# A state-space and attention kernel: softplus as one ScalarE function over three tiles in PSUM, and two changes to the order of work

## The chip, the core and the metric

The kernel runs on one core of one Trainium2 chip. The core has five engines that run side by side, each with its own queue of instructions in fixed order: TensorE (PE in the profile), VectorE (DVE), ScalarE (ACT), GpSimd (POOL) and SyncE (SP, which here only starts DMA transfers). The metric is the device time of one execution in microseconds (us). Three runs of the kernel before took 4100.95, 4101.35 and 4101.04 us, median 4101.04.

## The reference

The input is a batch of 8 images of 384 channels and 32 x 32 pixels, that is 1,024 positions. Layer 0 normalises each position over the channels, runs a selective state-space model (Mamba) forwards and backwards along the positions with the same weights, adds a gated depthwise 3 x 3 convolution, and adds the input. Layer 1 is causal attention with six heads over the 1,024 positions, and a feed-forward with sign-binarised weights and 8-bit scaling by groups of the batch. The groups cover five of the eight images; the feed-forward adds nothing for the rest.

What the change touches is delta, the step width of the state-space model:

```
dt, Bm, Cm = jnp.split(x_dbl, [dt_rank, dt_rank + D_STATE], axis=-1)
delta = jax.nn.softplus(jnp.einsum('blr,dr->bld', dt, dt_proj_w) + dt_proj_b)
A = -jnp.exp(A_log)
deltaA = jnp.exp(delta[..., None] * A)
deltaBu = (delta * u)[..., None] * Bm[:, :, None, :]
# step: h = dA * h + dBu; y = sum over 16 states of h * c
```

softplus(x) is log(1 + exp(x)). The rank of dt is 24, the number of states is 16, and everything is computed in 32-bit floats.

## The kernel before, in words

Channels lie on the 128 partitions in three chunks (`c`), positions along the free dimension in two halves of 512 (`h`), and `d` is the direction. A tile of 128 x 512 floats fills one of the eight banks of PSUM. One bank is for sums of the scan (`ps_y`), two for the scan's decay factors (`ps_da`), and five (`ps_any`) are shared by all else. In SBUF, ten tiles of 128 x 1,024 (`mid`) and six of three times that size (`big`) are shared in turn.

**The stages.** For each batch element `before_scan` (L639) normalises, projects, convolves, applies Silu, keeps u and the rows of B and C in DRAM, and computes the gates and the local convolution. Its last steps are the deltas (L903). For each of the four pairs of direction and half (`parts_of`) and each chunk, a delta step loads u from DRAM, makes one matmul of 25 rows (24 of dt, one that brings in the bias) into a bank `dp`, and works out softplus as max(x, 0) + log(1 + exp(-|x|)), with a correction for what is lost when 1 is added to a small number. That takes six instructions of ScalarE (Abs, Exp, add 1, Ln, a copy of w = 1 + e into the bank, and a copy of the result to SBUF) and four of VectorE. It then writes delta (`dl`) and delta times u (`ud`) to DRAM. There are 12 such steps for one batch element and 96 in all.

The scan itself is cut into units (L940): one unit is two blocks of 32 channels times 4 states for one chunk, one pair of direction and half, 96 units for one batch element. A unit (`s_first`, `s_scan`, `s_sum`) is a GpSimd multiplication of `scan_ud` and a row of B into `scan_g` (six buffers), then twice an Exp on ScalarE into `ps_da` and a recurrence on VectorE, a ScalarE copy of the last column (`scan_carry`) in half of the units, a GpSimd multiplication by the row of C, and TensorE sums over the states into `ps_y`. When all units of a chunk are through, `s_gate` puts u, the two directions and z together. Then come attention (L1068) and, for five batch elements, the feed-forward (L1375).

**What sets the order.** The code doesn't call the engines directly. Each call is recorded as an operation with a rank, which is its number in the order of recording, less an offset (`hurry`); a `together` block is recorded as one operation, so its instructions stand one behind another on their engine. `place` (L246) then plays the operations through with estimated costs: at each moment an engine takes the ready operation of the lowest rank whose tiles can be given a place. What comes out is the fixed order of every engine's queue. Waits on the chip follow from data and buffers. All instructions are emitted at L364, so the profile shows this line for nearly all; tiles tell them apart.

The order of recording comes from the end of the function. `slots` (L1505) records the scan's units with an offset of 600. `spread_over` (L1493) merges lists of steps, each with a weight in us, by the share of its list's weight that lies ahead of a step. The first batch element's first part runs alone (`lead`). The rest of it, the second and third elements' `before_scan` and the binarising of the weights are merged with the first units. From then on a cycle is attention of element i, then its feed-forward merged with `before_scan` of element i + 3 (L1571). The units are laid over this sequence so that an element's units are through before its attention.

[...] The kernel keeps the set named in `LOG_EXP` (L52), which has Exp and Ln; wherever it uses Silu, Tanh or Gelu, it records them together and asks for `LOG_EXP` again right after (L861, L1425).

Of the kernel before, what the change touches and what calls it, by code (L numbers as in the profile page):

```python
# [22 lines left out]
HB = 512  # L23
# [3 lines left out]
RANK = 24  # L27
# [13 lines left out]
DW = BC0 + 2 * NS  # L41
# [10 lines left out]
LOG_EXP = "natural_log_exp_and_others"  # L52
# [108 lines left out]
class Plan:  # L161
# [15 lines left out]
    @contextmanager  # L177
    def together(self):
        self.group = []
        yield  # L180
        self.group = None

    @contextmanager
    def hurry(self, offset):
        self.sooner += offset
        yield
        self.sooner -= offset
# [58 lines left out]
    def place(self):  # L246
        engines = self.ENGINES
        waiting = {e: [] for e in engines}
        ready = {e: [] for e in engines}
        free_at = {e: 0.0 for e in engines}  # L250
        count = itertools.count()
# [42 lines left out]
        while events:  # L294
            now = events[0][0]
            while events and events[0][0] <= now:
                heapq.heappop(events)
            moved = True
            while moved:
                moved = False  # L300
                for e in engines:
                    while waiting[e] and waiting[e][0][0] <= now:
                        op = heapq.heappop(waiting[e])[2]
                        if op.start is None:
                            heapq.heappush(ready[e], (op.rank, next(count), op))
                    while free_at[e] <= now and ready[e]:
                        aside, op, held = [], None, set()
                        while ready[e]:
                            item = heapq.heappop(ready[e])
                            if item[2].start is not None:  # L310
                                continue
                            if fits(item[2], now, held):
                                op = item[2]
                                break
                            aside.append(item)
                        for item in aside:
                            heapq.heappush(ready[e], item)
                        if op is None:
                            break
                        op.name, op.start, moved = e, now, True  # L320
                        for t in op.tiles:
                            if t.place is None:
                                k = t.kind
                                k.free.sort()
                                t.place = k.free.pop(0)[1]
                        if op.dma:
                            free_at[e] = now + 0.06
                            dma_free = max(dma_free, now + 1.2) + op.time
                            op.end = dma_free + 1.2
                        else:  # L330
                            op.end = free_at[e] = now + op.time
                        heapq.heappush(events, (free_at[e], next(count), e))
                        done.append(op)
                        for t in op.tiles:
                            users_left[id(t)] -= 1
                            if not users_left[id(t)]:
                                at = max(u.end for u in t.users) + self.SIGNAL
                                t.kind.free.append((at, t.place))
                                t.kind.freed += 1
                                heapq.heappush(events, (at, next(count), e))  # L340
                        for nxt in op.behind:
                            nxt.left -= 1
                            if not nxt.left:
                                release(nxt)
# [33 lines left out]
def kernel(  # L378
# [21 lines left out]
    nc = plan = Plan(tc, homes)  # L400
    together, hurry = plan.together, plan.hurry
# [6 lines left out]
    dram = Pool(plan, "dram", 5, DRAM)  # L408
    ps = Pool(plan, "ps", 1, PSUM)

    def ctile(name, shape, dt=F32):
        return const.tile(shape, dt, name=name, tag=name)
# [4 lines left out]
    def mtile(name, n=L):  # L417
        return mid.tile([P, n], F32, name=name, tag="mid")
# [6 lines left out]
    def bank(name, tag=None):  # L425
        tag = tag if tag in BANKS else "any"
        return ps.tile([P, HB], F32, name=name, tag=tag, bufs=BANKS[tag])

    def parts_of(b):
        return LAST_PARTS if b == ORDER[-1] else PARTS  # L430

    def half(h):
        return slice(h * HB, (h + 1) * HB)

    def chunk(c):
        return slice(c * P, (c + 1) * P)

    def load(dst, src):
        nc.sync.dma_start(out=dst, in_=src)
# [8 lines left out]
    spilled = {}  # L448
# [16 lines left out]
    wdt = ctile("wdt", [P, C])  # L465
    for d in range(2):
        nc.scalar.dma_start(out=wdt[d * DW : d * DW + RANK, :], in_=w_dt)
        nc.scalar.dma_start(
            out=wdt[d * DW + RANK : d * DW + RANK + 1, :],
            in_=vecs[:, V_DTB : V_DTB + 1].rearrange("c o -> o c"),  # L470
# [19 lines left out]
    nc.vector.tensor_copy(cmask[:, HB - P :], masked)  # L490
    onesc = ctile("onesc", [P, P])
    nc.gpsimd.memset(onesc, 1.0 / C)
    onecol = ctile("onecol", [P, 1])
    nc.gpsimd.memset(onecol, 1.0)
    eps = ctile("eps", [P, 2])
    nc.gpsimd.memset(eps[:, 0:1], 1e-6)
    nc.gpsimd.memset(eps[:, 1:2], 1e-5)
# [141 lines left out]
    def before_scan(b, tags, emit, later=None, diags=None, lead=None):  # L639


        st = {}
        turns = itertools.cycle(tags)

        def bank_of(name):
            return bank(name, next(turns))
# [253 lines left out]

        def delta(c, d, h):  # L903
            ew = mtile(f"ew{d}_{b}_{c}_{h}").rearrange("p (i l) -> p i l", i=2)
            du = mtile(f"du{d}_{b}_{c}_{h}").rearrange("p (i l) -> p i l", i=2)
            e, w, dl, u = ew[:, 0, :], ew[:, 1, :], du[:, 0, :], du[:, 1, :]
            load(u, spilled[b, "u", d, c][:, half(h)])
            dp = bank_of(f"dp{d}_{b}_{c}_{h}")
            r = slice(d * DW, d * DW + RANK + 1)
            nc.tensor.matmul(  # L910
                out=dp, lhsT=wdt[r, chunk(c)], rhs=st["xd"][r, half(h)], start=True, stop=True
            )
            nc.scalar.activation(e, dp, AF.Abs)
            nc.scalar.activation(e, e, AF.Exp, scale=-1.0)
            nc.scalar.activation(w, e, AF.Identity, bias=onecol)
            nc.scalar.activation(dl, w, AF.Ln)

            nc.vector.scalar_tensor_tensor(dl, dp, 0.0, dl, ALU.max, ALU.add)
            nc.scalar.copy(dp, w)
            nc.vector.scalar_tensor_tensor(dp, dp, 1.0, e, ALU.subtract, ALU.subtract)  # L920
            nc.vector.tensor_tensor(dp, dl, dp, ALU.subtract)
            nc.vector.tensor_tensor(u, u, dp, ALU.mult)
            nc.scalar.copy(dl, dp)
            for i, what in enumerate(("dl", "ud")):
                t = dram.tile([P, HB], F32, name=f"s{what}_{d}_{b}_{c}_{h}", tag=f"sp_{what}_{d}_{c}_{h}")
                nc.sync.dma_start(out=t, in_=du[:, i, :])
                spilled[b, what, d, c, h] = t

        for d, h in parts_of(b):
            for c in range(NC):  # L930
                to = lead if lead is not None and (d, h) == (0, 0) else emit
                to(lambda c=c, d=d, h=h: delta(c, d, h), 3.0)

# [556 lines left out]
    class Gap(float):  # L1490
        pass

    def spread_over(*lists):  # L1493

        keyed = []
        for k, steps in enumerate(lists):
            total, at = sum(us for _, us in steps), 0.0
            for f, us in steps:
                keyed.append(((at + us / 2) / total, k, (f, us)))
                at += us  # L1500
        return [e[2] for e in sorted(keyed, key=lambda e: e[:2])]

# [22 lines left out]
    def run(*lists):  # L1525
        for f, _ in spread_over(*lists):
            f()

    def steps_of(stage, *args, **kwargs):
        out = Steps()  # L1530
        stage(*args, out, **kwargs)
        return out
# [31 lines left out]
    rest, later, due = [], list(ORDER[1 + ahead :]), [(0.0, 0)]  # L1564
    for i, b in enumerate(ORDER):
        if i > 0:
            due.append((sum(us for _, us in rest), i * per))
        fed = Steps()
        rest += steps_of(attention, b, fed) if i < B - 1 else []
        if fed and later:  # L1570
            fed = spread_over(fed, steps_of(before_scan, later.pop(0), ("pt", "pt", "av")))  # L1571
            fed = [(f, JOINT * (SHORT if isinstance(us, Gap) else us)) for f, us in fed]
        rest += fed
        if i == B - 2:
            late, early = Steps(), Steps()
            attention(ORDER[-1], Steps(), late, early)
            due.append((sum(us for _, us in rest), i * per + 3 * per // len(PARTS)))
            rest += early
# [7 lines left out]
    at = 0.0  # L1586
# [61 lines left out]
```

## Time and profile before

| | |
|---|---|
| median of three runs | 4101.04 us |
| profiled execution | 4101.66 us |
| its span, first to last instruction | 4099.8 us |
| mean granted TensorE clock | 0.894 |
| PE, DVE busy | 3414.5, 3458.9 us |
| ACT, POOL busy | 2687.2, 3577.0 us |
| DMA | 612.03 MB, 149 GB/s |
| first multiplication of GpSimd for the scan | 74.7 us |
| last one ends | 3921 us |

The span is that of one profiled execution; the execution's own time is 1.9 us longer. Busy time of an engine is the time in which it executes; the rest it waits, for data, for a buffer or for the instruction ahead in its own queue. Rows of groups read: line, engine, operation, output from inputs (partitions x elements), count, then busy time in us and mean in ns of one, and after the second bar the time that the engine stood idle just ahead of these instructions, and for whom. Rows of waits read: engine, waiting tile, whom it waited for, total us, number of waits, longest.

### The profile page before, as it was taken

Reading aid. Unit: us, or ns where it says so; the run is one execution under the profiler, and the core shown is the slowest. Engines: PE = TensorE matmul, PEld = TensorE weight load, DVE = VectorE, ACT = ScalarE, POOL = GpSimd, SP = SyncE. Lnnn points to the kernel's source line nnn. Section 1 sums busy time; section 2 is a strip of 40 time slices with the busy share of each in tenths; the row PEclk is TensorE's granted clock in tenths of the full one; section 3 lists DMA queues with packets and bytes.
Section 4 is the critical chain, followed back from the end, with each engine's and each line's share of the span. In section 5 each row is a group of like instructions: output and inputs, shape, how many; then the busy total and the mean of one; then the engine's idle time right before and its main releaser. Section 6 shows DMA issues by size and latency. Waiting matters only on the chain. (4 is left out here: it accounts for less than half of the span.)

```text
span 4099.8 us, 43593 instructions
## 1 busy us (share of the span) xinstructions
PE 3414.5 (83%) x12426; PEld 1336.9 (33%) x12426; DVE 3458.9 (84%) x4867; ACT 2687.2 (66%) x5288; POOL 3577.0 (87%) x1560
## 2 busy tenths in 40 slices
PE   4557387989889898979998798987989879998999
PEld 1112022433323333324333243332433323333344
DVE  5999999888898889988899977999788998877843
ACT  5856767586674867657666667666586665856635
POOL 3999999999799997989998899978899788999920
PEclk8678596999979999889999899997999979999999
DMA  5635655333374344543345633447324464233300
GB/s 195 218 134 189 237 176 209 131 108 133 136 243 146 104 142 146 196 166 115 127 140 174 223 114 115 136 143 268 114 79 133 148 240 169 96 128 110 133 26 31
DMA packets 338971, 612.03 MB, mean 149 GB/s; under 512 B 34617, under 2 KB 93417, under 8 KB 338729
## 3 DMA queue, kind: packets, MB, share of 16 engines
q1 hardware_dynamic: 329072, 593.10, 42.0%
q10 hardware_dynamic: 9656, 16.15, 1.1%
q8 instruction: 98, 1.61, 0.2%
q14 instruction: 145, 1.18, 0.1%
HBM read 456.03 MB, written 153.09 MB: 149 GB/s over the span
## 5 line engine op out<-in xcount | busy, mean ns | idle before, releaser
L364 POOL TENSOR_TENSOR scan_g<-scan_g,scan_bc 128x1024 f32<-128x1024 f32 x768 | 1814.8, 2368 | 199.3 <-ACT scan_carry L364 116.8
L364 POOL TENSOR_TENSOR scan_g<-scan_ud,scan_bc 128x1024 f32<-128x1024 f32 x768 | 1820.0, 2377 | 140.5 <-DMA scan_ud<-dram_sp_ud 68.4
L364 ACT ACTIVATE ps_da<-scan_dl,const_amat 128x512 f32<-128x512 f32 x1536 | 1050.2, 689 | 702.1 <-DVE scan_g L364 688.5
L364 DVE TENSOR_TENSOR_SCAN scan_g<-ps_da,scan_carry,scan_g 128x512 f32<-128x512 f32 x768 | 943.3, 1267 | 99.1 <-POOL scan_g L364 81.2
L364 DVE TENSOR_TENSOR_SCAN scan_g<-ps_da,scan_g 128x512 f32<-128x512 f32 x768 | 898.0, 1208 | 108.4 <-POOL scan_g L364 83.5
L364 PE MATMUL ps_any<-big_big,mid_mid 128*128 128x512 f32 x2016 | 940.9, 619 | 38.5 <-DVE big_big L364 18.4
L364 PE MATMUL ps_y<-scan_g,const_gather 128*32 128x512 f32 x3072 | 477.6, 698 | 299.7 <-POOL scan_g L364 293.9
L364 PEld LDWEIGHTS ps_any<-big_big,mid_mid 128*128 128x128 f32 x2016 | 384.9, 197 | 598.0 <-issue 481.0
L364 PE MATMUL ps_any<-big_big,big_big 128*128 128x512 f32 (+4 forms) x1728 | 558.6, 560 | 22.3 <-ACT ptp_ptn L364 7.4
L364 PE MATMUL ps_any<-const_ident,mid_mid 128*128 128x128 f32 x1728 | 306.7, 306 | 61.9 <-DVE small_nm L364 25.2
L364 DVE CUSTOM_DVE_ANT_0 mid_mid<-ps_any,const_cmask 128x512 f32<-128x512 f32 (+3 forms) x576 | 292.2, 547 | 59.5 <-PE ps_any L364 58.9
L364 PEld LDWEIGHTS ps_any<-big_big,big_big 64*128 64x128 f32 (+1 forms) x1728 | 226.9, 190 | 322.3 <-issue 202.2
L364 DVE SCALAR_TENSOR_TENSOR ps_any<-big_big,const_vec,ps_any 128x496 f32<-128x496 f32 (+6 forms) x420 | 303.2, 727 | 19.1 <-ACT ps_any L364 5.5
L364 PEld LDWEIGHTS ps_any<-const_ident,mid_mid 128*128 128x128 f32 x1728 | 200.1, 150 | 283.8 <-issue 89.1
L364 ACT COPY ptp_ptn<-ps_any 128x512 f32<-128x512 f32 (+3 forms) x576 | 256.2, 478 | 48.9 <-PE ps_any L364 41.1
L364 ACT ACTIVATE mid_mid<-mid_mid,small_low 128x512 f32<-128x512 f32 (+3 forms) x384 | 242.8, 635 | 53.5 <-DVE small_low L364 52.9
L364 PE MATMUL ps_any<-ptp_ptn,big_big 128*64 128x512 f32 (+3 forms) x1152 | 260.6, 532 | 13.1 <-ACT ptp_ptn L364 11.8
L364 PEld LDWEIGHTS ps_y<-scan_g,const_gather 128*32 128x32 f32 x3072 | 64.5, 115 | 595.1 <-POOL scan_g L364 499.4
L364 PE MATMUL ps_any<-mid_mid,const_wdt 25*128 25x512 f32 x192 | 155.3, 939 | 81.5 <-ACT mid_mid L364 51.6
L364 ACT ACTIVATE mid_mid<-mid_mid 128x512 f32<-128x512 f32 (+1 forms) x261 | 188.8, 738 | 3.9
L364 ACT COPY mid_mid<-ps_any 128x512 f32<-128x512 f32 x234 | 134.6, 581 | 79.3 <-DVE mid_mid L364 38.0
L364 PE MATMUL ps_any<-mid_mid,const_onesc 128*128 128x512 f32 x252 | 135.2, 665 | 57.7 <-ACT mid_mid L364 45.3
(106 smaller groups left out, 3467.6 us busy)
## 6 DMA issues: line engine op xcount, KB each, us to landing
scan_ud<-dram_sp_ud SPq DMA_DIRECT2D x384, 256.0 KB, 3.6
scan_dl<-dram_sp_dl SPq DMA_DIRECT2D x384, 256.0 KB, 3.5
scan_bc<-dram_rows SPq DMA_DIRECT2D x256, 256.0 KB, 3.2
scan_us<-dram_sp_u SPq DMA_DIRECT2D x96, 256.0 KB, 2.6
mid_mid<-dram_sp_u SPq DMA_DIRECT2D x96, 256.0 KB, 4.6
dram_sp_ud<-mid_mid SPq DMA_DIRECT2D x96, 256.0 KB, 3.7
dram_sp_dl<-mid_mid SPq DMA_DIRECT2D x96, 256.0 KB, 3.2
dram_sp_u<-mid_mid SPq DMA_DIRECT2D x42, 512.0 KB, 5.1
```

Source lines behind the costliest of these rows:

```text
L364: getattr(engine, what)(*[mapped(v) for v in args], **{k: mapped(v) for k, v in kwargs.items()})
```

## The change

There are four parts.

1. `delta` becomes `deltas`, one step for three chunks: three loads of u and three matmuls into three banks; then, as one `together` group with an offset of 60, three Softplus activations in place in the banks and the request for `LOG_EXP`; then for each chunk one VectorE multiplication by u, one ScalarE copy and the two transfers to DRAM. The tile `ew` and the constant `onecol` go. A step's weight is 6.0 for three chunks, where it was 3.0 for each.
2. In `place`, an operation of any engine but TensorE that touches a PSUM tile which already has its place is queued with a rank lower by 60.
3. `spread_over` can multiply the shares of all lists but the first by a factor `sooner`.
4. The merge of the feed-forward with the later element's `before_scan` uses `sooner=0.8`.

```diff
@@ place
                         if op.start is None:
-                            heapq.heappush(ready[e], (op.rank, next(count), op))
+                            opened = e != "tensor" and any(
+                                t.place is not None and t.kind.space == PSUM for t in op.tiles
+                            )
+                            heapq.heappush(ready[e], (op.rank - 60 * opened, next(count), op))
@@ before_scan
-        def delta(c, d, h):
-            ew = mtile(f"ew{d}_{b}_{c}_{h}").rearrange("p (i l) -> p i l", i=2)
-            du = mtile(f"du{d}_{b}_{c}_{h}").rearrange("p (i l) -> p i l", i=2)
-            e, w, dl, u = ew[:, 0, :], ew[:, 1, :], du[:, 0, :], du[:, 1, :]
-            load(u, spilled[b, "u", d, c][:, half(h)])
-            dp = bank_of(f"dp{d}_{b}_{c}_{h}")
-            r = slice(d * DW, d * DW + RANK + 1)
-            nc.tensor.matmul(
-                out=dp, lhsT=wdt[r, chunk(c)], rhs=st["xd"][r, half(h)], start=True, stop=True
-            )
-            nc.scalar.activation(e, dp, AF.Abs)
-            nc.scalar.activation(e, e, AF.Exp, scale=-1.0)
-            nc.scalar.activation(w, e, AF.Identity, bias=onecol)
-            nc.scalar.activation(dl, w, AF.Ln)
-
-            nc.vector.scalar_tensor_tensor(dl, dp, 0.0, dl, ALU.max, ALU.add)
-            nc.scalar.copy(dp, w)
-            nc.vector.scalar_tensor_tensor(dp, dp, 1.0, e, ALU.subtract, ALU.subtract)
-            nc.vector.tensor_tensor(dp, dl, dp, ALU.subtract)
-            nc.vector.tensor_tensor(u, u, dp, ALU.mult)
-            nc.scalar.copy(dl, dp)
...
+        def deltas(d, h):
+            st_of = []
+            for c in range(NC):
+                du = mtile(f"du{d}_{b}_{c}_{h}").rearrange("p (i l) -> p i l", i=2)
+                load(du[:, 1, :], spilled[b, "u", d, c][:, half(h)])
+                dp = bank_of(f"dp{d}_{b}_{c}_{h}")
+                r = slice(d * DW, d * DW + RANK + 1)
+                nc.tensor.matmul(
+                    out=dp, lhsT=wdt[r, chunk(c)], rhs=st["xd"][r, half(h)], start=True, stop=True
+                )
+                st_of.append((c, du, dp))
+            with hurry(offset=60), together():
+                for _, _, dp in st_of:
+                    nc.scalar.activation(dp, dp, AF.Softplus)
+                nc.scalar.preload_act_table_set(LOG_EXP)
+            for c, du, dp in st_of:
+                dl, u = du[:, 0, :], du[:, 1, :]
+                nc.vector.tensor_tensor(u, u, dp, ALU.mult)
+                nc.scalar.copy(dl, dp)
...
         for d, h in parts_of(b):
-            for c in range(NC):
-                to = lead if lead is not None and (d, h) == (0, 0) else emit
-                to(lambda c=c, d=d, h=h: delta(c, d, h), 3.0)
+            to = lead if lead is not None and (d, h) == (0, 0) else emit
+            to(lambda d=d, h=h: deltas(d, h), 6.0)
@@ spread_over
-    def spread_over(*lists):
+    def spread_over(*lists, sooner=1.0):
...
-                keyed.append(((at + us / 2) / total, k, (f, us)))
+                share = (at + us / 2) / total
+                keyed.append((share * sooner if k else share, k, (f, us)))
@@ the cycles
-            fed = spread_over(fed, steps_of(before_scan, later.pop(0), ("pt", "pt", "av")))
+            fed = spread_over(fed, steps_of(before_scan, later.pop(0), ("pt", "pt", "av")), sooner=0.8)
```

More of the change, by code (lines that the diff above doesn't have):

```diff
@@ L492 @@
     nc.gpsimd.memset(onesc, 1.0 / C)
-    onecol = ctile("onecol", [P, 1])
-    nc.gpsimd.memset(onecol, 1.0)
     eps = ctile("eps", [P, 2])
@@ L899, in _ @@
                 spilled[b, "rows", d] = rows
-        def delta(c, d, h):
-            ew = mtile(f"ew{d}_{b}_{c}_{h}").rearrange("p (i l) -> p i l", i=2)
-            du = mtile(f"du{d}_{b}_{c}_{h}").rearrange("p (i l) -> p i l", i=2)
-            e, w, dl, u = ew[:, 0, :], ew[:, 1, :], du[:, 0, :], du[:, 1, :]
-            load(u, spilled[b, "u", d, c][:, half(h)])
-            dp = bank_of(f"dp{d}_{b}_{c}_{h}")
-            r = slice(d * DW, d * DW + RANK + 1)
-            nc.tensor.matmul(
-                out=dp, lhsT=wdt[r, chunk(c)], rhs=st["xd"][r, half(h)], start=True, stop=True
-            )
-            nc.scalar.activation(e, dp, AF.Abs)
-            nc.scalar.activation(e, e, AF.Exp, scale=-1.0)
-            nc.scalar.activation(w, e, AF.Identity, bias=onecol)
-            nc.scalar.activation(dl, w, AF.Ln)
-            nc.vector.scalar_tensor_tensor(dl, dp, 0.0, dl, ALU.max, ALU.add)
-            nc.scalar.copy(dp, w)
-            nc.vector.scalar_tensor_tensor(dp, dp, 1.0, e, ALU.subtract, ALU.subtract)
-            nc.vector.tensor_tensor(dp, dl, dp, ALU.subtract)
-            nc.vector.tensor_tensor(u, u, dp, ALU.mult)
-            nc.scalar.copy(dl, dp)
[L924 to L927, printed above, removed]
@@ new lines, in deltas @@
+        def deltas(d, h):
[17 more added lines that the diff above has]
+                nc.scalar.copy(dl, dp)
+                for i, what in enumerate(("dl", "ud")):
+                    t = dram.tile(
+                        [P, HB], F32, name=f"s{what}_{d}_{b}_{c}_{h}", tag=f"sp_{what}_{d}_{c}_{h}"
+                    )
+                    nc.sync.dma_start(out=t, in_=du[:, i, :])
+                    spilled[b, what, d, c, h] = t
```

## The prediction

> **What bounds the kernel now.** I read the busy shares first, then the busy time by stage, then who makes GpSimd wait, then the groups of instructions that the edit touches, and last the start of the run.
>
> ```profile
> PE 3414.5 (83%) x12426; PEld 1336.9 (33%) x12426; DVE 3458.9 (84%) x4867; ACT 2687.2 (66%) x5288; POOL 3577.0 (87%) x1560
> POOL 3999999999799997989998899978899788999920
> ```
>
> No engine is full, and three are near it. GpSimd (POOL) runs the two multiplications of every scan unit, 1,536 of them; the slices say that it is full in long stretches and has dips. By stage (columns: busy us, with instruction counts, of PE, weight loads, DVE, ACT, POOL; then TensorE clock, DMA share, GB/s):
>
> ```profile
> 75.00:740.00 665.00, 414.88 (x1142) 127.47 (x1141) 616.24 (x737) 457.87 (x779) 632.73 (x274) 0.72 0.54 189
> 740.00:3450.00 2710.00, 2365.11 (x8470) 931.90 (x8469) 2376.53 (x3252) 1813.55 (x3509) 2469.50 (x1062) 0.92 0.44 151
> 3450.00:3921.00 471.00, 429.79 (x1988) 183.62 (x1987) 371.10 (x624) 304.13 (x723) 465.65 (x202) 0.96 0.35 120
> 3921.00:4100.00 179.00, 168.95 (x768) 80.57 (x766) 67.64 (x206) 79.17 (x227) 0.54 (x1) 1.00 0.08 26
> ...
> 1150.00:1250.00 100.00, 77.93 (x192) 25.95 (x191) 94.52 (x115) 69.76 (x116) 88.89 (x40) 0.76 0.75 260
> 1250.00:1350.00 100.00, 94.66 (x358) 40.56 (x356) 81.43 (x132) 57.73 (x134) 94.44 (x41) 0.99 0.38 130
> ```
>
> The end is: head (75 us until POOL's first multiplication), POOL's 3,568 us, the idle time in between, and 179 us after its last one. So POOL's idle time is what can be won: 665.00 - 632.73 = 32 us in the first stage, 2,710.00 - 2,469.50 = 240 us in the five cycles of attention, feed-forward and before_scan, 5 us after 3,450. The fifth row is a stretch with twelve delta steps: DVE is at 95% and POOL at 89%, and PE falls to 78% at a clock of 0.76. A stretch of attention (750 to 950 us) has POOL idle for 0.4 us only. Who makes POOL wait between 740 and 3,450 us:
>
> ```profile
> POOL scan_g L364 <- ACT scan_carry L364: 104.4, 51, 13.8
> POOL scan_g L364 <- PE ps_y L364: 62.4, 25, 7.6
> POOL scan_g L364 <- DVE scan_g L364: 59.4, 34, 9.1
> ```
>
> The first and third are one thing: the scan of a unit (Exp on ACT, recurrence on DVE, a copy of the carry on ACT) is late. The second is PE: the sums that free scan_g stand behind other matmuls.
>
> **What the Trainium skill says.** "Perfetto Trace Analysis", section Optimization Strategy, says that a kernel can have several regimes, each with its own most contended engine; the rows above agree (DVE first in the delta stretch, POOL in attention, PE in the tail). "ScalarE activation tables", section What a function is on this engine, says that the same operands cost the same whichever function's table is read; the trace agrees for Exp and Ln (one row, 628 ns) and doesn't show Softplus. "ScalarE: Activation LUTs", section What ACT_TABLE_LOAD costs, gives 1,283 ns for a load and about as much again for a drain; here a load takes 1,283 ns, and at 103.40 us the next ACTIVATE starts 1.30 us after it, so I count no drain. "TensorE: Matmul & The Clock Gate", section What's actually happening, says that idle stretches halve the array's clock; the delta row's 0.76 against 0.99 right after agrees.
>
> **The change part by part.** The rows concerned, of all 96 delta steps (the first also holds nothing else: 96 Exp and 96 Ln):
>
> ```profile
> L364 ACT ACTIVATE mid_mid<-mid_mid 128x512 f32<-128x512 f32 x192 | 120.5, 628 | 3.7
> L364 ACT ACTIVATE mid_mid<-mid_mid,const_onecol 128x512 f32<-128x512 f32 x96 | 69.1, 720 | 2.4 <-PE ps_any L364 0.9
> L364 ACT ACTIVATE mid_mid<-ps_any 128x512 f32<-128x512 f32 x96 | 56.5, 588 | 25.5 <-PE ps_any L364 13.9 <-DVE ps_any L364 7.8 <-DMA big_big<-dram_sp_gy 3.7
> L364 ACT COPY ps_any<-mid_mid 128x512 f32<-128x512 f32 x96 | 55.6, 580 | 22.1 <-DVE mid_mid L364 21.8
> L364 ACT ACT_TABLE_LOAD x67 | 86.0, 1283 | 1.8 <-PEq L1635 0.7
> L364 DVE TENSOR_TENSOR ps_any<-mid_mid,ps_any 128x512 f32<-128x512 f32 x96 | 66.6, 694 | 2.9
> L364 DVE SCALAR_TENSOR_TENSOR ps_any<-ps_any,mid_mid 128x512 f32<-128x512 f32 x96 | 65.4, 681 | 8.4 <-ACT ps_any L364 7.8
> ```
>
> DVE: three of four operations go: 0.694 + 0.681 + 0.677 (max and add, the row of mid_mid from ps_any and mid_mid) = 2.052 us a step, 24.6 us a batch, 197 us in all. ACT: Abs 0.588, Exp and Ln 2 x 0.628, Identity 0.720, copy into the bank 0.580 = 3.144 us go; one Softplus comes, never seen in the trace. Bounds 0.55 to 0.72, the cheapest and dearest 512-wide form; I take 0.578, what Exp over a bank in place (ps_any from ps_any) takes. Three steps save 7.70 us and get two table loads, 2.57: net 5.13 us a group, 20.5 a batch, 164 in all. The loads are a choice too: the diff reloads the log-and-exp set itself, so Softplus lies in another; if it didn't, 82 us of ACT more would be saved.
>
> Matmuls, the 96 loads of u and the 192 spills on SP stay; the three loads of a group now stand ahead of its six spills. One mid tile a step goes (ew), which only relieves its ten buffers. Three of the five shared banks are held together; I cost it at nothing, because the old steps already overlapped (at 1,201 us one step's Abs runs ahead of the last copy of the one before) and each bank is held for no longer than the old chain's 6 us; without that cover, a group holds back the next bank user for its 4.3 us. The removed memset is 0.1 us under the loads at the start.
>
> *Head.* Before, POOL's first load stands on SP behind the third step's dl spill:
>
> ```profile
> 70.51 0.32 SPq L364 DMA_DIRECT2D dram_sp_dl<-mid_mid  x1
> 70.92 2.46 SPq L364 DMA_DIRECT2D scan_ud<-dram_sp_ud  x4
> 74.70 11.59 POOL L364 TENSOR_TENSOR scan_g<-scan_ud,scan_bc 128x1024 f32<-128x1024 f32 x5 [61.64 <-DMA scan_ud<-dram_sp_ud]
> ```
>
> The six matmul records of the three steps end at 56.4. After: last Softplus 57.0, reload 58.3, three copies 59.9, spill 60.3, load landing 3.8 later: 64.3 instead of 74.7. Of these 10 us I take 8, as the first units then meet the next batch's convolutions on DVE.
>
> *First stage.* 33 more steps take 68 us of DVE out of 665; POOL can win at most its 32 us. I take half: 15 us.
>
> *Five cycles.* A cycle has 240 / 5 = 48 us of POOL idle. About 10 stand behind the four Gelu of 2.85 us (waits of 9.4 and 13.8 us at two of them), which stay; 12 are PE's ps_y. The twelve delta steps' stretch and the 100 us after it hold 17 to 28 us of the idle (11 + 6 in the rows shown). DVE loses 24.6 us of work there; I put it at 20 us of POOL idle a cycle: 100 us. Bounds: 0 (the scans then wait for ACT or PE) and 26 (all but Gelu and PE): 130.
>
> *New bursts.* A group blocks ACT for 1.28 + 3 x 0.58 + 1.28 = 4.3 us, and queued behind it are a unit's Exp and carry copy, for which DVE and then POOL wait. A Silu burst of 4.2 us at 103.40 costs POOL nothing (no idle from 98 to 185 us). The Gelu burst of 13.7 us cost 9.4, so some 4 us are covered. Where DVE is behind already, the cover is gone: 0 to 4.3 us each. I take 0.5 x 32 = 16 us.
>
> *Planner and placing.* An operation that reads or writes a bank already given gets 60 ranks; scans stand 600 ahead, so it mainly reorders evictions among the rest: 0, bounds -15 (banks sooner free for PE) to +15. The before_scan list counts 180 us of weight before and 168 after, with deltas in its last 36 and 24; with the factor 0.8 they move from shares 0.80 to 1.00 of the feed-forward to 0.69 to 0.80, and the convolutions and gates ahead of them are packed tighter, where DVE is full (184.5 of 200 us from 950 to 1,150). What DVE saves pays for it: 0, bounds -20 to +40. SP's loads and spills of the moved steps move along; a batch's deltas are ready before its scan in either case (the last spill of a delta is issued at 3,394 us).
>
> *Tail.* PE is busy for 169 of 179 us; nothing there is edited: 0.
>
> Sum: -8 - 15 - 100 + 16 = -107 us. The profiled execution took 4,101.66 us for a span of 4,099.8; span 3,993, execution 3,995. The median of the runs is 0.6 below the profiled one: **3,994 us**.
>
> **The rivals.** *Only off the path* (B): POOL's waits in the delta stretch pass to PE's sums and to the bursts; what is left is head, half the first stage and 5 us a cycle, 8 + 8 + 25 = 41 us: 4,060 (4,045 to 4,092). For it: 62 us of waits are PE's, and PE already runs at 87% over the cycles; against: PE loses 22 us in the delta row for want of ACT and DVE. *Slower* (C): the bursts. They fall where DVE is behind, so each stalls POOL by its length and delays the next scan; from 3.8 us a group (123 / 32) on they eat the gain, and with the tighter placing at its +40 it ends near 4,140 (4.3 x 32 + 40 - 123 = +55 at most). For it: the waits of 9.4 and 13.8 us behind Gelu; against: the Silu burst at 103. *More* (D): the rest of the work also gets ahead of the scans, so that part of the last batch's early half leaves the tail; 60 us in the first stage and 25 a cycle are there for it, and 179 us can lose some 60: 3,915. *Not what it says*: Softplus without loads, or the planner not moving the list; it changes the sum by less than 40 us and lies in A.
>
> **How the numbers follow.** My forecast (A, 3,945 to 4,045) has 0.60, B 0.18, D 0.08, C 0.11, and no difference 0.03. Within 0.2%, 8 us, is about what can't be told from no change. Faster is A, B and D: 0.86. The range leaves out C, no change and the lower half of D, 0.18: 3,925 to 4,092, which also takes in the bounds of the cycles and of the placing.
>
> **What would show it.** Softplus of about 0.58 us x96 and 131 table loads; DVE near 3,262 and ACT near 2,523 us; POOL's first multiplication near 65 us; POOL idle from there to its last below 200 us (now 277), with the fall in the delta stretches; the tail at 179. I am wrong if POOL's waits on scan_carry grow, with table loads right ahead of them, or if ps_y waits take what DVE's gave up.

## The result, and the profile after

The changed kernel takes 4044.70 us (median of four runs, 4043.55 to 4048.24), where the kernel before takes 4101.19 us beside it (4100.95 to 4103.24). The ratio is 0.9863, with a 95% interval of 0.9846 to 0.9880: 56.5 us faster, about half of the 107 us forecast. The time lies at the edge of the forecast's own range and inside the wider one. The profiled execution took 4048.24 us with a span of 4046.4 us, 53.4 us below the span before.

The busy shares and GpSimd's slices after:

```profile
PE 3387.3 (84%) x12426; PEld 1330.0 (33%) x12426; DVE 3264.4 (81%) x4580; ACT 2546.6 (63%) x4967; POOL 3570.8 (88%) x1559
POOL 2999999999999999789998799987899997999910
```

DVE fell by 194.5 us (forecast 197). The slices show where GpSimd gained: the first 7 stands in slice 17 of 40, where it stood in slice 11; later dips remain. By stage, with the limits of the stages 50 to 60 us sooner, as the work behind the first stage is (columns as in the prediction):

```profile
75.00:690.00 615.00, 423.81 (x1170) 140.05 (x1171) 527.91 (x615) 393.28 (x644) 594.76 (x258) 0.75 0.59 202
690.00:3400.00 2710.00, 2343.55 (x8486) 923.10 (x8485) 2275.17 (x3093) 1733.96 (x3324) 2511.85 (x1083) 0.92 0.45 152
3400.00:3861.00 461.00, 405.86 (x1920) 169.10 (x1919) 359.47 (x611) 300.68 (x715) 455.37 (x197) 0.96 0.35 116
3861.00:4047.00 186.00, 174.91 (x782) 83.16 (x780) 69.12 (x209) 79.26 (x227) 0.28 (x1) 1.00 0.07 25
...
1090.00:1190.00 100.00, 95.85 (x263) 35.06 (x262) 72.99 (x80) 53.78 (x82) 100.00 (x44) 0.91 0.75 259
```

GpSimd's idle time in the first stage is 615.00 - 594.76 = 20 us (before 32), in the five cycles 2,710.00 - 2,511.85 = 198 us (before 240), and behind 3,400 us 461.00 - 455.37 = 6 us: 224 us in all, where the prediction's sign was "below 200". In the delta stretch of the first cycle, the fifth row, the bound moved as forecast: DVE 73 us where it had 95, GpSimd full, the TensorE clock 0.91 where it was 0.76. In the later cycles most of what is won there is lost again, as shown below. GpSimd's waits between 690 and 3,400 us:

```profile
POOL scan_g L367 <- PE ps_y L367: 90.7, 22, 12.5
POOL scan_g L367 <- ACT scan_carry L367: 54.5, 36, 8.1
POOL scan_g L367 <- DVE scan_g L367: 38.7, 21, 10.9
```

The lateness of the scan (second and third rows) fell from 163.8 to 93.2 us. The wait for PE's sums rose from 62.4 to 90.7 us: 28 of the 71 us came back as another wait.

To see when this happens I split GpSimd's timeline by batch element, 192 multiplications each, and added up the idle time ahead of them (us). In the first element's sum, some 62 us are the wait for the first load in both kernels.

| | el. 0 | 1 | 2 | 3 | 4 | 5 | 6 | 7 | sum |
|---|---|---|---|---|---|---|---|---|---|
| idle before | 82 | 12 | 47 | 54 | 44 | 49 | 51 | 0 | 339 |
| idle after | 80 | 2 | 15 | 43 | 50 | 48 | 42 | 3 | 283 |
| of it for ps_y, before | 0 | 0 | 6 | 20 | 13 | 15 | 13 | 0 | 67 |
| of it for ps_y, after | 3 | 0 | 0 | 23 | 24 | 28 | 18 | 0 | 96 |

42 of the 56 us are won in elements 1 and 2, which are scanned from 538 to 1,446 us. From element 3 on, the idle time is what it was, and the wait for ps_y makes up more of it. The length of a cycle agrees: from the first Gelu to the fifth it takes (3,238.0 - 1,089.8) / 4 = 537 us before and (3,211.1 - 1,054.7) / 4 = 539 us after. GpSimd's last multiplication ends at 3,861.3 us instead of 3,921.5, and what follows it takes 185.1 instead of 178.3 us: -60.2 + 6.8 = -53.4 us, the difference of the spans.

### The profile page after: what moved, and what is told of

Its sections match the earlier page's. It is cut to its first block, busy times and chain, and to the rows that moved or that the text cites. A ratio compares the mean times of both kernels' runs of the same rounds, so it can differ in the third digit from the quotient of the medians.

```text
span 4046.4 us, 42961 instructions
## 1 busy us (share of the span) xinstructions
PE 3387.3 (84%) x12426; PEld 1330.0 (33%) x12426; DVE 3264.4 (81%) x4580; ACT 2546.6 (63%) x4967; POOL 3570.8 (88%) x1559
## 5 line engine op out<-in xcount | busy, mean ns | idle before, releaser
L367 PE MATMUL ps_any<-big_big,mid_mid 128*128 128x512 f32 x2016 | 952.9, 625 | 78.4 <-DVE big_big L367 56.5
L367 PE MATMUL ps_y<-scan_g,const_gather 128*32 128x512 f32 x3072 | 467.8, 686 | 275.1 <-POOL scan_g L367 265.0
L367 PE MATMUL ps_any<-mid_mid,const_wdt 25*128 25x512 f32 x192 | 132.1, 852 | 41.6 <-DVE mid_mid L367 32.2
L367 DVE COPY big_big<-ps_any 128x512 f32<-128x512 f32 (+1 forms) x86 | 54.2, 631 | 128.6 <-PE ps_any L367 128.6
```

Of the source, the lines that this page charges most:

```text
L367: getattr(engine, what)(*[mapped(v) for v in args], **{k: mapped(v) for k, v in kwargs.items()})
```

## The experiments

Each kernel was run beside the kernel before; times are medians. "Idle" is GpSimd's idle time counted as above. A kernel with another edit also gets another order of its queues from `place`; what that alone can do is measured below (29 us), and differences under it can't be laid to an edit.

**Which part carries it.** Four kernels take the change apart. `d_only` has the Softplus part alone; its edits of the changed kernel:

```
- heapq.heappush(ready[e], (op.rank - 60 * opened, next(count), op))
+ heapq.heappush(ready[e], (op.rank - 0 * opened, next(count), op))
...
- fed = spread_over(fed, steps_of(before_scan, later.pop(0), ("pt", "pt", "av")), sooner=0.8)
+ fed = spread_over(fed, steps_of(before_scan, later.pop(0), ("pt", "pt", "av")), sooner=1.0)
```

> The kernel after with only its first part: Softplus over three tiles, no lowering of ranks, factor 1.0. Theory PACK (the factor 0.8 packs before_scan ahead of Gelu, where DVE is full, and loses there what Softplus saves behind it): about 4,015 us, 30 faster than after, the distance from one Gelu to the next near 525 us instead of 537 to 539. Theory PACE (the cycle of 537 us is set by something that neither Softplus nor the order touches, such as the pace of the scans): 4,045 us, distance unchanged. Theory HELP (rank and factor each add to the gain): 4,060 us or more.

`d_opened` has Softplus and the ranks (the second of these edits alone), `d_sooner` has Softplus and the placing (the first alone):

> The kernel after with the factor 1.0 instead of 0.8. PACK: 4,010 to 4,020 us, GpSimd's waits for PE's sums fall from 97 us toward 67, the windows with PE below 35 of 50 us ahead of Gelu go. PACE: 4,045 us. HELP: 4,055 us.

> The kernel after without the lowering of ranks for taken banks. PACK and PACE: 4,045 us within 10, the ranks only reorder evictions. HELP: 4,055 us or more.

`order_only` is the kernel before with both changes of order and the old delta steps:

> The kernel before with both order changes (ranks lower by 60 on taken banks, factor 0.8) and its own softplus. PACK: slower than before, 4,115 to 4,130 us, since the packing has nothing to pay for it. PACE: 4,100 us. HELP: 4,080 us.

| kernel | us | ratio to before, 95% |
|---|---|---|
| d_only | 4050.19 | 0.9873, 0.9860 to 0.9887 |
| d_opened | 4049.59 | 0.9870, 0.9856 to 0.9883 |
| d_sooner | 4074.41 | 0.9930, 0.9917 to 0.9944 |
| order_only | 4111.22 | 1.0020, 1.0013 to 1.0027 |

Softplus alone gives 52 of the 56.5 us; with both changes of order in place on either side (`order_only` against the changed kernel) it gives about 65. The two changes of order bring 5 us on top, which the intervals can't tell from nothing; without Softplus they cost 9. Beside Softplus the ranks alone change nothing in the time, and the factor alone costs 24 us. The prediction's nought for the two, with bounds from -35 to +55, stands. None of the three theories in these expectations has the time right in all four; PACE has the unchanged distance from one Gelu to the next right, 538 us in `d_only`.

**Where Softplus acts.** `d_first` uses the new delta steps for the first three batch elements only, `d_later` for the other five only (with `not in` for `in`); the rest keeps the old `delta`. Both are edits of `d_only`:

```
- to(lambda d=d, h=h: deltas(d, h), 6.0)
+ if b in ORDER[:3]:
+     to(lambda d=d, h=h: deltas(d, h), 6.0)
+     continue
+ for c in range(NC):
+     to(lambda c=c, d=d, h=h: delta(c, d, h), 3.0)
```

> Softplus over three tiles for the first three batch elements only, the old delta steps for the other five; order of work as before. The prediction's own sum gives 8 + 15 - 6 = 17 us for these: about 4,085. Theory FRONT (the five later cycles give nothing, because PE's waits take over there what DVE and ACT give up; the gain is all in the part before the cycles): 4,055 us, nearly the whole 52 of the first part alone.

> The opposite: old delta steps for the first three elements, Softplus for the other five. The prediction's sum: 100 - 10 = 90 us faster, 4,012. FRONT: within 12 us of before, 4,090 to 4,100.

`d_first` takes 4069.89 us, 31.9 below before (ratio 0.9921, 0.9909 to 0.9934); `d_later` 4092.48 us, 9.3 below (0.9977, 0.9968 to 0.9986). Idle in elements 0 to 2 is 106 us with `d_first` (before 141) and 143 with `d_later`; in elements 3 to 7 it is 199 and 192 (before 198). In these runs 60 of the 96 steps, those of the five cycles, gain 9 us, and the 36 of the first stage 32 us, which show up as less idle time in elements 1 and 2. FRONT was right for `d_later`; for `d_first` its 4,055 was 15 us too low, and the prediction's own 4,085 was 15 too high. Some 11 us come only from both together, and no run assigns them. 9 and 11 us are less than order alone can do (below); that the cycles' steps don't bring 100 us is beyond it. GpSimd's waits from 740 to 3,450 us in `d_later`:

```profile
POOL scan_g L367 <- PE ps_y L367: 116.8, 20, 27.6
POOL scan_g L367 <- ACT scan_carry L367: 54.4, 23, 11.8
POOL scan_g L367 <- DVE scan_g L367: 51.8, 26, 10.4
```

In the same window the kernel before has 104.4 + 59.4 us of lateness and 62.4 us for ps_y. With the cycles' own deltas 58 us go from the first and 54 us come to the second: almost all of it is handed on. The other kernels agree. GpSimd's waits for ps_y sum to 44 to 70 us over the whole run in the four kernels with old delta steps in the cycles, and to 86 to 122 us in the ten with Softplus there.

The traces also tell where in a cycle this happens. GpSimd's idle time (us), summed over the second to the fifth cycle, by distance from the start of Gelu:

| | 100 us ahead to 100 behind | 100 to 300 behind | of the latter for ps_y |
|---|---|---|---|
| before | 123 | 76 | 31 |
| d_only | 53 | 139 | 89 |
| after | 82 | 106 | 81 |

In the rest of a cycle GpSimd is never idle. The sums of the four stretches from 100 to 300 us behind Gelu, the kernel before first, then `d_only` (POOL last before the semicolon; 800 us less it is the idle time):

```profile
sum 800.00, PE 667.89 PEld 266.70 DVE 692.07 ACT 514.91 POOL 724.51; mean PE 166.97 PEld 66.68 DVE 173.02 ACT 128.73 POOL 181.13
sum 800.00, PE 662.47 PEld 273.92 DVE 617.19 ACT 456.13 POOL 660.95; mean PE 165.62 PEld 68.48 DVE 154.30 ACT 114.03 POOL 165.24
```

So around Gelu GpSimd does get back 70 us in `d_only`, 17 a cycle, about the size of the forecast's 20 but mostly ahead of the delta steps. In the next 200 us it loses 63 of them again, most of it waiting for PE's sums. In the place where the forecast had put the gain, the delta steps and the 100 us behind them, idle time in these four cycles is 96 us before, 138 in `d_only` and 108 after.

**The bursts.** The prediction charged the new table loads 16 us. `d_burst` is `d_only` with two more table loads in every group, so that a group blocks ACT for 6.7 us instead of 4.2 (medians of the 32 groups):

```
  for _, _, dp in st_of:
      nc.scalar.activation(dp, dp, AF.Softplus)
+ nc.scalar.preload_act_table_set("exp_and_others")
+ nc.scalar.preload_act_table_set("exp_and_friends")
  nc.scalar.preload_act_table_set(LOG_EXP)
```

> The first part alone (Softplus everywhere, order as before) with two more table loads behind the three Softplus of each group: 64 loads more, 82 us of ScalarE, and a block of 6.9 us instead of 4.3. The prediction puts 0.5 us on a block of 4.3; if blocks are covered by GpSimd's slack: at most 15 us over the 4,050 of the first part alone. If ScalarE's time is on the path: 50 to 82 us more.

It takes 4040.59 us (0.9850, 0.9836 to 0.9863), 10 us less than `d_only`. ACT is busy for 2624.9 us, 82 more. ACT's timeline in one group:

```profile
1167.78 3.86 ACT L367 ACT_TABLE_LOAD   x3
```

Around it GpSimd has no idle time from 1,157.7 to 1,173.9 us. In the changed kernel a group looks so (ACT's timeline), and GpSimd runs without a gap beside this one as well:

```profile
1099.23 1.28 ACT L367 ACT_TABLE_LOAD   x1
1100.53 1.56 ACT L367 ACTIVATE ps_any<-ps_any 128x512 f32<-128x512 f32 x3
1102.11 1.28 ACT L367 ACT_TABLE_LOAD   x1
```

Not all bursts are like these two. From the start of a burst to 6 us behind its end, and without the group in the head, GpSimd's idle time adds up to 20 us in the changed kernel, 34 in `d_only` and 72 in `d_burst`, where 24 of the 31 have some. So longer bursts do leave gaps beside them, but the whole run isn't longer: the idle time of all elements is 277 us in `d_burst` and 292 in `d_only`. The 82 us more of ACT's time are not on the path as a whole; a few us can hide in what order does. Nor are the 10 us a gain from the loads; the run on mere order, below, shows what such a difference is worth.

**Is it the room for the sums?** Since GpSimd now waits for ps_y, which frees scan_g, `a_g7` gives the changed kernel a seventh scan_g buffer. The space comes from two constants (one column of ones broadcast, and the mask built in wv's tile before wv is loaded):

```
- g = sp.tile([P, 2, HB], F32, name=f"g_{u.name}", tag="g", bufs=6)
+ g = sp.tile([P, 2, HB], F32, name=f"g_{u.name}", tag="g", bufs=7)
...
- onesc = ctile("onesc", [P, P])
+ onesc = ctile("onesc", [P, 1])
  nc.gpsimd.memset(onesc, 1.0 / C)
+ onesc = onesc.to_broadcast([P, P])
```

> The kernel after with seven scan_g buffers instead of six (room made by a one-column constant and by building the mask in a weight tile). If GpSimd's 97 us of waits for PE's sums are a matter of free buffers: these waits below 60 us and 4,015 to 4,030 us. If PE is behind over whole stretches, one buffer only moves the wait: 4,040 to 4,048 us.

It takes 4033.47 us (0.9834, 0.9821 to 0.9848), 11 us less than the changed kernel and the least of all. But the waits for ps_y hardly move, 85.8 us from 690 to 3,400 where they were 90.7, so one more buffer doesn't take them away, and 11 us is not more than a mere change of order can bring (below). Neither forecast came true: one had the waits below 60 us, the other the time at 4,040 or more.

**Is it PE's work?** In the cycles PE is busy for 86% of the time. `b_w2h` and `d_w2h` are the kernel before and `d_only` with every second term of the feed-forward's second product left out, 180 calls or 360 records of the trace less (each of these calls leaves two records):

```
- for k in range(NF):
+ for k in range(0, NF, 2):
...
- stop=(k == NF - 1),
+ stop=(k == NF - 2),
```

> The kernel before with half of the second feed-forward product left out (6 of 12 matmuls for each output tile, 36 of 72 for a batch element), so that TensorE has some 33 us less to do in each of the five cycles, all of it behind Gelu, where the deltas lie. If the deltas' stretch of before was set by VectorE and ScalarE: little faster, 4,070 to 4,095 us. It is the pair of d_w2h.

> The first part of the change alone (Softplus, order as before), with the same half of the second product left out. Theory PE FLOOR (behind Gelu the 72 matmuls of this product are the next bound, and that is why Softplus gains nothing in the cycles): the distance to b_w2h grows from 52 us to 90 or more. Theory DVE ELSEWHERE (the cycle's length is set ahead of Gelu, where VectorE is full with work that Softplus doesn't touch): the distance stays at 45 to 60 us.

Both got slower: 4124.30 us (1.0052, 1.0038 to 1.0066) and 4063.48 us (0.9907, 0.9892 to 0.9922; `d_only` has 0.9873). Their distance is 60.8 us, where it is 52.4 with the whole product. PE's busy time fell from 3414.5 to 3293.0 us, and its mean clock from 0.894 to 0.871. The first was forecast faster and wasn't. A floor set by this product would have made the distance 90 us or more; 8 us of growth speak against it, and the 60.8 lie just above the 45 to 60 of the other theory. As both kernels also have a new order of their queues, this excludes a large floor only.

**How much is mere order?** `d_cost` is `d_only` with a smaller estimate for a table load in the planner. No instruction of the program is added or removed; the order of the queues changes, and one copy out of PSUM moves from ACT to DVE.

```
  if what == "preload_act_table_set":
-     return 2.8
+     return 1.3
```

> The first part of the change alone, with the planner told 1.3 us for a table load instead of 2.8 (the trace has 1.283): no instruction changes, only the order in which the planner puts them. It shows how far a reordering without any other reason moves the time. If the 10 us between d_only and d_burst are only that: within 12 us of 4,050 on either side. If they come from something that the two more loads do, 4,050 within 4.

It takes 4079.19 us (0.9940, 0.9926 to 0.9954), 29 us more than `d_only`, where at most 12 were expected. So a difference of 10 to 30 us between two kernels of different order can't be laid to the edit itself: not the 10 us that `d_burst` gains, nor the 24 us that `d_sooner` loses, nor the 11 us of `a_g7`. The 52 us of Softplus are beyond it, the 32 us of `d_first` just beyond, the 9 us of `d_later` within. The eight kernels with Softplus everywhere and the whole feed-forward take 4,033 to 4,079 us, the two with none 4,101 and 4,111: in no order tried does Softplus fail to gain, but its size goes with the order.

**What ends the lead.** The waits for ps_y look so in `d_only`: first PE's timeline, then GpSimd's.

```profile
2287.10 30.20 PE L367 MATMUL ps_any<-big_big,big_big 128*128 128x512 f32 x70
2317.14 14.35 PE L367 MATMUL ps_any<-const_wv,big_big 128*128 128x384 f32 x44
2331.43 1.07 PE L367 MATMUL ps_y<-scan_g,const_gather 128*32 128x512 f32 x8
```

```profile
2332.61 9.34 POOL L367 TENSOR_TENSOR scan_g<-scan_ud,scan_bc 128x1024 f32<-128x1024 f32 x4 [27.62 <-PE ps_y L367]
```

114 records of matmuls of the feed-forward and of the next attention stand in PE's fixed queue ahead of eight of sums; PE is not idle but busy with something else, and GpSimd, idle from 2,305 us on, waits 27.6 us for sums that take 1.1. This order is the planner's, made from ranks and estimated times. The scan's operations are recorded with an offset of 600 ranks; the theory is that the scan goes first as long as this lead over the work around it lasts, in the first elements, and has to share once it is used up. `d_lead` gives it more, `d_only` with an offset of 1,000 ranks instead of 600:

```
  def ahead_of_all(k):
-     with hurry(offset=600):
+     with hurry(offset=1000):
```

> The first part of the change alone (Softplus, order as before), with the scan units recorded 1,000 ranks ahead instead of 600. Theory LEAD (the units run faster than the rest and use up their lead in ranks; from then on sums, Exp and recurrences stand behind older work of the rest, and GpSimd's idle time is what holds the two together, so Softplus pays only as long as the lead lasts, in the first three elements): the lead lasts about an element longer, GpSimd's idle time in the scan of the fourth element falls from 41 us to 15 or less, some more in the fifth, and the time to 4,000 to 4,025 us. Theory TAIL (the end is set by the rest anyway): the idle time falls just so, but the stretch after GpSimd's last multiplication grows from 178 us by the same, 4,045 to 4,055. If the lead has nothing to do with it: idle 41 and 4,050 as in the first part alone, give or take the 30 us that a mere reordering moved.

It takes 4075.02 us (0.9933, 0.9920 to 0.9947), 25 us more than `d_only`. GpSimd's idle time in element 3 falls from 41 to 12 us, and the waits for ps_y from 690 to 3,400 us from 87.2 to 62.0. Its last multiplication ends at 3,835 us, 35 us sooner. But the stretch after it grows (windows by stage, `d_only` first, then `d_lead`):

```profile
3870.60:4049.00 178.40, 168.40 (x767) 80.53 (x766) 67.67 (x206) 79.20 (x227) 0.00 (x0) 1.00 0.07 26
```

```profile
3835.00:4069.00 234.00, 222.52 (x948) 104.60 (x948) 81.21 (x227) 92.20 (x257) 0.15 (x1) 1.00 0.10 34
```

181 more matmul records, 222.52 - 168.40 = 54 us of PE's time, lie behind the scan. In this kernel, what the scan took from the shared engines was taken from the rest: the sixth attention starts its scores at 3,458 us instead of 3,415. LEAD was right on the idle time of element 3 and wrong on the time; TAIL was right that the end grows, but it grew by 55 us and not by 35. As the 25 us in all are within what order does, the exchange is shown and its net cost isn't. It isn't a law for every order either: `d_burst` has 26 us less idle time in elements 3 to 7 than `d_only`, with the same stretch at the end and a shorter time (table).

All kernels in one table. The last two columns are the end of GpSimd's last multiplication and what is left of the span after it, in the profiled execution:

| kernel | us | idle el. 0-2 | idle el. 3-7 | last ends | after it |
|---|---|---|---|---|---|
| before | 4101.19 | 141 | 198 | 3921.5 | 178.3 |
| after | 4044.70 | 97 | 186 | 3861.3 | 185.1 |
| d_only | 4050.19 | 99 | 193 | 3870.6 | 178.2 |
| d_opened | 4049.59 | 89 | 185 | 3861.9 | 185.2 |
| d_sooner | 4074.41 | 111 | 210 | 3906.3 | 178.3 |
| order_only | 4111.22 | 163 | 184 | 3929.4 | 179.0 |
| d_first | 4069.89 | 106 | 199 | 3890.5 | 178.3 |
| d_later | 4092.48 | 143 | 192 | 3913.6 | 178.2 |
| d_burst | 4040.59 | 110 | 167 | 3860.8 | 178.3 |
| a_g7 | 4033.47 | 90 | 186 | 3855.6 | 175.6 |
| b_w2h | 4124.30 | 145 | 219 | 3944.3 | 178.2 |
| d_w2h | 4063.48 | 99 | 206 | 3883.4 | 178.3 |
| d_cost | 4079.19 | 115 | 198 | 3899.6 | 178.3 |
| d_lead | 4075.02 | 94 | 155 | 3835.2 | 233.7 |

The profiled execution of `d_sooner` took 4086.35 us, 12 more than its median; in the others it is within 5 us. In `after` and `d_opened`, which have the ranks, the stretch behind the scan is 7 us longer and the scan's end 9 us sooner than in `d_only`; `a_g7` and `order_only` have the ranks too, and their stretches are 175.6 and 179.0 us. The kernel with the least idle time in elements 3 to 7, `d_lead`, is also the one with the longest stretch at the end.

## Why the prediction was right or wrong

**Right: direction, range and arithmetic of instructions.** That 4044.70 us lies within the 3,945 to 4,045 of the forecast itself is a matter of 0.3 us, and in part luck: 16 us charged for the bursts made up for some of the 58 us missing in the cycles. The mechanism was nearer to that of rival B, whose 4,045 to 4,092 begin just above. Softplus is not in the set of function tables that has Exp and Ln, as the prediction chose: the program has a table load ahead of each of the 32 groups and one behind it. The groups of ScalarE after the change:

```profile
L367 ACT ACT_TABLE_LOAD x131 | 168.1, 1283 | 2.9 <-PEq L1636 0.7
L367 ACT ACTIVATE ps_any<-ps_any 128x512 f32<-128x512 f32 x138 | 75.0, 581 | 13.1 <-PE ps_any L367 11.7
```

131 loads were forecast, 67 + 2 x 32. The second row holds 42 Exp at 578 ns from before and 96 Softplus: (138 x 581 - 42 x 578) / 96 = 582 ns, forecast 578. What "ScalarE activation tables", section What a function is on this engine, in the Trainium skill says of equal cost is thereby shown for Softplus too. DVE's 3264.4 us were forecast as 3,262. ACT's 2546.6 were forecast as 2,523: the durations of its instructions, added up, fell by 161 us (3,016 to 2,855), close to the 164 worked out, but busy time counts overlapping neighbours once and fell by 141.

**Wrong: "I put it at 20 us of POOL idle a cycle: 100 us".** This is the step that failed, and nearly all of the error. Over the cycles' window the idle time fell by 240 - 198 = 42 us, and even most of these come from steps of the first stage: 32 of them lie in element 2, and `d_first`, with old steps in the cycles, has 29. The run with the cycles' own steps alone gains 9 us (`d_later`), or 2 us a cycle. A relief of about that size is there, 17 us a cycle around Gelu in `d_only`, mostly ahead of the delta steps. What failed is to take it for the gain of the whole cycle: the prediction held the waits for PE at 12 us a cycle and counted no new ones, though its own lower bound of 0 ("the scans then wait for ACT or PE") named them; they took back nearly all of it in the next 200 us. `d_later` shows the waits on the scan falling by 58 us and those for ps_y rising by 54. The sentence that closes the prediction named just this, "if ps_y waits take what DVE's gave up", and rival B said it as well; B's 5 us a cycle was nearer. Why the waits pass on is shown in part: other matmuls stand ahead of the sums in PE's queue, and `d_lead` moves the waits by the ranks, with more work left at the end. How much of GpSimd's idle time in the later cycles an order could win is open; less DVE work alone hardly won any.

**Too small: "I take half: 15 us" for the first stage.** By place it was nearly right, 32 - 20 = 12 us. By cause it was too small: the 36 delta steps up to there are worth 32 us (`d_first`), of which most appears as idle time that elements 1 and 2 no longer have. The prediction had counted only the idle time inside the stage itself. With the steps saved there the work behind starts sooner, the first Gelu of `d_first` at 1,038.0 instead of 1,089.8 us; that element 2 waits less because of this was not tested apart.

**Wrong: "64.3 instead of 74.7" in the head.** GpSimd's first multiplication starts at 74.76 us, as before. SP's queue after the change:

```profile
60.42 0.33 SPq L367 DMA_DIRECT2D dram_sp_dl<-mid_mid  x1
...
63.42 0.61 SPq L367 DMA_DIRECT2D dram_sp_ud<-mid_mid  x1
64.50 0.32 SPq L367 DMA_DIRECT2D dram_sp_u<-big_big  x1
65.45 0.98 SPq L367 DMA_DIRECT2D dram_sp_u<-mid_mid  x2
66.48 2.66 SPq L367 DMA_DIRECT2D scan_dl<-dram_sp_dl  x4
69.19 2.54 SPq L367 DMA_DIRECT2D scan_ud<-dram_sp_ud  x4
```

The six spills are issued by 64.0 us, where before the third dl spill alone stood at 70.5. Then come three spills of the next element's u, which wait for its Silu, and the four loads of scan_dl, which stood behind scan_ud before. Together they take the 5 us from 64.5 to 69.2, and the load that is then issued lands 5.6 us later instead of 3.8. The step followed the data and left out that the planner sorts SP's queue anew: 8 us were counted, none came.

**Wrong: 16 us for the bursts.** `d_burst` made them 2.6 us longer each and got no slower. For the whole run the bound of 0 was the nearer one, though some bursts do have idle time beside them. Rival C's stall of GpSimd by the length of each burst isn't seen. The planner's and the placing's 0 stand (5 us together, not told apart from 0), and of the tail's 0, 6.8 us were missed; no run shows what makes it longer, since of four kernels with the ranks two have it and two don't.

By place, the balance is: head 0, first stage -12, cycles -42, tail +7. With -6 us of GpSimd's busy time this makes -53, against a span that is 53.4 us shorter.

**Left open.** What sets the 537 us of a cycle isn't settled: not GpSimd alone, since its idle time there persists; nor, for the larger part, the feed-forward's second product, by `b_w2h` and `d_w2h`. The obvious rival is VectorE ahead of Gelu: in the five stretches of 50 us that end at a Gelu, DVE is busy for 240 of 250 us before and for 246 after, while PE falls from 229 to 133 us and GpSimd rises from 200 to 240. No run takes work off DVE there, so this stays untested. Why less work on PE made both kernels slower isn't shown either: the lower clock is measured, but a new order of the queues is in these runs too, and their 13 and 21 us lie within what order does in `d_cost`.

## What to carry to other kernels

Where several engines share work in queues of fixed order, the idle time of the fullest engine is not all there to be won: ask for each stretch which other work uses the engines in that time, and whether it has to be done anyhow. Follow a relief to the end of the cycle before it is counted: here 70 us of idle time went and 63 came back in the next 200 us, mostly as another wait. The same steps gained more in the start-up stage than in the steady cycles (32 us from 36 steps, 9 us from 60, the latter within the noise of order). And before a small part of a planned kernel is judged by its time, a run with the same instructions in another order tells how large a difference has to be: here 29 us of 4,050.

## What the runs showed of the hardware

A burst of two table loads and three Softplus takes ACT 4.2 us, with the next ACTIVATE 1.30 us after a load's start, and three loads in direct sequence take 3.86 us, 1.29 us each. "ScalarE: Activation LUTs", section What ACT_TABLE_LOAD costs, gives 2.66 us for a switch with its drain; a drain is not seen in these bursts, and the measurement decides. Softplus over 128 x 512 floats in PSUM takes 582 ns where Exp takes 578. With 360 matmul records of the feed-forward less, TensorE's mean granted clock was 0.871 instead of 0.894, PE was busy for 121.5 us less, and the kernel took 21 us more; its queues also had another order.
